# Attention, convolution and a routed expert block on one core: routing split in two parts, an early store tied to a turn, and two projections that change places

## The chip, the core and the metric

The kernel runs on one core of one Trainium2 chip. The metric is the device time of one execution in microseconds (us); less is better. Engines go by their names in the profile: PE (TensorE, the matmuls), PEld (its weight loads), DVE (VectorE), ACT (ScalarE), POOL (GpSimd), SP (SyncE, which here only issues DMAs).

## The reference, cut to what matters

`x` has 8 sequences ("batches" below) of 512 tokens with 256 values each. All data are float32.

```python
x = x + attn_block(layernorm(x))
    # q, k, v = projections; ctx = causal softmax attention, 16 heads of 16
    # q2 = conv1d(ctx, width 3); ctx2 = causal attention(q2, k, v); out projection
x = x + ffn_block(layernorm(x))

def ffn_block(x):
    h = x + attention(rmsnorm(x))            # rotary causal attention, 16 heads of 16
    t = rmsnorm(h)
    probs = softmax(t @ w_router)            # 8 experts
    topw, topi = top_k(probs, 2); topw /= sum(topw)
    return h + sum over the two experts of topw * expert(t)   # silu(t wg) * (t wu) @ wd, hidden 704
```

So each batch passes three causal attentions, and each token then goes to its two best experts.

## The kernel before, in words

**Tiles and stages.** A batch is 4 tiles of 128 tokens. The eight batches are taken in four pairs, p = 0 to 3 (batches 2p and 2p+1). A pair runs six attentions one after the other: first, second, third attention, each for the one batch and then for the other. One attention is 9 steps. A step is 16 score matmuls into two PSUM tiles `sc` (line 1212), two exponentials on ACT from `sc` to `pr` (L1219), the causal mask on POOL (L1227), and, some steps later, the products with the values (L1142). There are only two `sc` tiles, so the scores of a step wait for the exponentials of the step before. After the last expert rows are known, a second phase runs the experts over sorted rows (L742 to L805).

**The order is written out by hand.** Two steps make a turn; a pair has 27 turns (`TURNS`), and turn t+k below is turn 27p+k. Everything that is not attention (projections, convolution, norms, routing) is a "unit" that `plan` puts into a turn. A turn emits: step A; due products with values; the mask; one row transfer (`send`); the "mid" follow-ups; the units of `small_units` and `first_units`; step B; its mask; a transfer; the "late" follow-ups; then the units of `units`; the "end" follow-ups. PE, ACT, DVE and POOL keep exactly that order in their queues. SP's order is left to a scheduler, which issues DMAs when it thinks they can start.

**Normalising an attention.** When a half (`ch`) of an attention has its sums in PSUM, ACT copies them (L1159), SP sends three DMAs (`r<-cs` twice, L1167; `cs<-cs`, L1168), and a turn later DVE does two reciprocals (L1172), two products (L1173) and, for a first attention, the four `differences` for the convolution (L1394 to L1397). For `ch` 0 that comes as a "mid" follow-up, ahead of `small_units`.

**Routing.** For a batch: `logits` (L1571) puts logits in PSUM and copies them to `lT` (L1579). `route` transposes them back (PE, L1585), and then is one chain on DVE: maximum and difference (L1593, L1594), the exponential on ACT (L1595), and then the sums, the two picks (`pick_largest`, L1240 to L1244), `both` (L1603) and the weights (L1604 to L1610). `slots` needs `both`: two matmuls (L1624, L1625) and 16 DVE instructions (L1627 to L1639). Routing of the batches of pair p-1 falls into pair p: `before0` in turns t+1 (`route`) and t+2 (`slots`), `before1` in t+7 and t+10. In t+2 the unit `h` follows `slots`: two groups of matmuls with `wo` (L1041), each followed by an addition on DVE (L1545), one on POOL (L1546) and two squares on ACT (L1548), which write into the same PSUM tile. All these PSUM tiles come from `mm_tile`, which has two banks and takes them in turn.

**The other units named here.** `k(ch)` is a projection (L1052) that ACT takes out of PSUM with two instructions (L1342); `values(half)` is one (L1070) that DVE takes out with two (L1088); both for the next batch, `next0`, in turns t+10 and t+11. `normed2` is ACT (L1480). `conv` is matmuls L1406 with L1415 on ACT and L1420, L1424 on DVE. `xn` (L1323) is the normalised input of the next batch; its transposes are L1292.

**Stores.** `store` (L1266) writes a batch's rows to `out`. For the last batch, 7, it is called early, in `stats` (turn t+20 of p = 2), before anything else touches `out` for that batch; its rows were loaded by a DMA (L679) that `fetch_next` of batch 6 issues (turn t+3 of p = 2).

## Time and profile before

| what | value |
|---|---|
| median of 3 runs | 1439.34 us (1436.92 to 1440.64) |
| the profiled execution: its time | 1439.65 us |
| its span in the trace | 1437.7 us |
| mean granted PE clock | 0.989 |
| PE busy | 1385.2 us, 96% |
| PE weight loads busy | 900.1 us, 63% |
| DVE, ACT, POOL busy | 734.2, 725.7, 579.7 us (51%, 50%, 40%) |
| mean busy share of DMA queues | 15.1% + 5.4% + 0.6% |

The profile is of one execution. Its span runs from the first to the last instruction; 1.95 us of the execution's time lie around it. Lines of the timeline give start, duration, engine, line, operation, tiles, and in brackets how long the engine was idle before and on whom it waited. Matmul ends are modelled, so a wait inside a group of matmuls counts as busy in part; the start of the next group tells the loss. "PEclk" in the table of stretches is the granted PE clock, as a share of full speed.

### The profile page before, as it was taken

To read this page: it belongs to the slowest core of one execution; us is meant where nothing else is said; L and a number is where in the kernel's file an instruction comes from. 1 tells how busy PE (TensorE), PEld (TensorE's weight loads), DVE (VectorE), ACT (ScalarE), POOL (GpSimd) and SP (SyncE) were. 2 spreads that over 40 slices of the span, in tenths; PEclk is the share of its full clock that TensorE was granted. 3 is DMA by queue.
4 is the path that set the end of the run, shared out by engine and by line. 5 is a ranking of instruction groups with operands and counts; after the bars stand their busy time and mean duration, and the time that the engine had idled before them with its cause. 6 is when DMAs were issued, how large, how long until landed. Compare 5 with 4: busy or idle time off the path is not lost. (4 is left out here: it accounts for less than half of the span.)

```text
span 1437.7 us, 32181 instructions
## 1 busy us (share of the span) xinstructions
PE 1385.2 (96%) x13476; PEld 900.1 (63%) x13476; DVE 734.2 (51%) x1458; ACT 725.7 (50%) x1175; POOL 579.7 (40%) x621
## 2 busy tenths in 40 slices
PE   8999999999999899999999999999999999999995
PEld 5566565666565566565565666666766767677673
DVE  5745877675977665976576855322222222222221
ACT  4777786776786676786776883211121111211110
POOL 3334333646333546333655345433324233332321
PEclk9999999999999999999999999999999999999998
DMA  5122122201001201010212022323131313232200
GB/s 148 58 89 83 60 85 69 83 32 57 13 32 45 94 35 58 13 51 31 100 60 71 24 78 101 124 63 112 45 108 61 97 60 103 76 98 81 82 20 17
DMA packets 62842, 97.63 MB, mean 68 GB/s; under 512 B 13516, under 2 KB 39064, under 8 KB 62688
## 3 DMA queue, kind: packets, MB, share of 16 engines
q1 hardware_dynamic: 52608, 69.74, 15.1%
q0 software_dynamic: 10080, 25.74, 5.4%
q8 instruction: 108, 1.77, 0.5%
q14 instruction: 46, 0.38, 0.1%
HBM read 46.06 MB, written 32.61 MB: 55 GB/s over the span
## 5 line engine op out<-in xcount | busy, mean ns | idle before, releaser
L1219 ACT ACTIVATE pr<-sc 128x1024 f32<-128x1024 f32 x432 | 418.8, 1023 | 153.0 <-PE sc L1212 149.3
L1227 POOL TENSOR_TENSOR pr<-pr,seen 128x512 f32<-128x512 f32 (+1 forms) x216 | 256.7, 1189 | 409.9 <-ACT pr L1219 409.8
L764 PE MATMUL pgu<-xgT,gu 128*128 128x384 f32 x1056 | 345.8, 487 | 2.2 <-DVE hT L779 1.6
L764 PEld LDWEIGHTS pgu<-xgT,gu 128*128 128x128 f32 x1056 | 200.0, 190 | 137.0 <-DVE hT L779 2.2
L778 ACT ACTIVATE sg<-pgu 128x384 f32<-128x384 f32 x120 | 58.8, 490 | 413.0 <-PE pgu L764 404.6
L1142 PE MATMUL av<-pr,va 64*32 64x512 f32 (+7 forms) x6144 | 218.9, 407 | 0.0
L1212 PE MATMUL sc<-qT,kT 32*128 32x320 f32 (+7 forms) x2048 | 192.4, 436 | 8.3 <-ACT pr L1219 6.2
L788 PE MATMUL po<-dn,hT 128*128 128x256 f32 x864 | 190.9, 379 | 2.0 <-issue 2.0
L779 DVE TENSOR_TENSOR hT<-sg,pgu 128x384 f32<-128x384 f32 x120 | 66.4, 554 | 247.2 <-ACT sg L778 243.2
L805 POOL DMA_INDIRECT out_dram<-so_far,xg x72 | 72.4, 1006 | 287.8 <-DVE so_far L795 222.1
L1172 DVE RECIPROCAL r<-r 128x256 f32<-128x256 f32 x96 | 167.5, 1744 | 20.5 <-DMA r<-cs 20.4
L1142 PEld LDWEIGHTS av<-pr,va 64*32 64x32 f32 x6144 | 113.4, 106 | 102.5 <-issue 73.7
L788 PEld LDWEIGHTS po<-dn,hT 128*128 128x128 f32 x864 | 162.4, 190 | 23.9 <-issue 2.4
L1212 PEld LDWEIGHTS sc<-qT,kT 32*128 32x128 f32 x2048 | 116.9, 184 | 82.7 <-ACT pr L1219 31.2
L795 DVE SCALAR_TENSOR_TENSOR so_far<-po,xg,so_far 128x256 f32<-128x256 f32 x72 | 34.8, 484 | 151.5 <-PE po L788 147.2
L1212 PE MATMUL sc<-q2T,kT 32*128 32x512 f32 (+7 forms) x1024 | 95.0, 434 | 1.3 <-ACT pr L1219 0.9
L750 POOL DMA_INDIRECT so_far<-out_dram,xg x72 | 74.0, 1028 | 53.7 <-issue 51.9
L1212 PEld LDWEIGHTS sc<-q2T,kT 32*128 32x128 f32 x1024 | 58.1, 184 | 34.5 <-issue 15.0
L1648 POOL DMA_INDIRECT xtab<-rows,slot x64 | 64.6, 1009 | 32.1 <-DVE pick L1637 15.6
L1052 PE MATMUL mm<-xT,wqkv_sb 128*128 128x512 f32 x128 | 62.7, 616 | 1.5 <-DVE xmT L1298 1.2
L1052 PE MATMUL mm<-xaT,wqkv_sb 128*128 128x512 f32 x128 | 61.3, 612 | 2.0 <-DVE xaT L1298 2.0
L1406 PE MATMUL mm<-terms,conv_sb 128*128 128x256 f32 x256 | 62.7, 390 | 0.0
(178 smaller groups left out, 1363.2 us busy)
## 6 DMA issues: line engine op xcount, KB each, us to landing
r<-cs SPq DMA_DIRECT2D x96, 128.0 KB
xtab<-pad SPq DMA_DIRECT2D x24, 397.5 KB
xg<-xtab SPq DMA_DIRECT2D x24, 397.5 KB
gu<-in_wg_dram SPq DMA_DIRECT2D x18, 352.0 KB
cs<-cs SPq DMA_DIRECT2D x48, 128.0 KB
dn<-in_wd_dram SPq DMA_DIRECT2D x9, 640.0 KB
gu<-in_wu_dram SPq DMA_DIRECT2D x18, 320.0 KB
out_dram<-x SPq DMA_DIRECT2D x9, 512.0 KB
```

The lines of the kernel that those rows point to most:

```text
L750: nc.gpsimd.indirect_dma_start(out=so_far[:, s, :], out_offset=None, in_=out, in_offset=token_of(xg, s), bounds_check=B * S - 1, oob_is_er ...
L764: nc.tensor.matmul(ps, gu[d][:, n0 : n0 + P], xgT[:, d, :], start=(d == 0), stop=(d == DC - 1),)
L779: nc.vector.tensor_mul(hT[k], sg, pu)
L788: nc.tensor.matmul(po, hT[k][:, s * P : (s + 1) * P], dn[:, k, :], start=(k == 0), stop=(k == NK - 1),)
L805: nc.gpsimd.indirect_dma_start(out=out, out_offset=token_of(xg, s), in_=so_far[:, s, :], in_offset=None, bounds_check=B * S - 1, oob_is_er ...
L1052: nc.tensor.matmul(ps, w[:, d, n0 : n0 + P], srcT[:, d, :S], start=(d == 0), stop=(d == DC - 1),)
L1142: nc.tensor.matmul(av[i][g * HP : (g + 1) * HP, j * KB :], v[rows, j, ch * G + g, :], pr[rows, g, at : at + n], start=(j == 0), stop=(j == ...
L1172: nc.vector.reciprocal(r[:, half], r[:, half])
L1212: nc.tensor.matmul(sc[:, g - g0, at : at + S - j * KB], kT[r0 : r0 + HP, ch, j], qT[r0 : r0 + HP, ch, j * KB : S], start=True, stop=True,)
L1219: nc.scalar.activation(pr[:, g0 : g0 + 2], sc, AF.Exp, scale=SCALE)
L1227: nc.gpsimd.tensor_tensor(diag, diag, seen.unsqueeze(1).unsqueeze(1).to_broadcast([P, G, len(parts), KB]), ALU.mult,).ins
L1648: nc.gpsimd.indirect_dma_start(out=xtab, out_offset=bass.IndirectOffsetOnAxis(ap=slot[:, c, k : k + 1], axis=0), in_=rows[:, c, :], in_off ...
```

## The change

Three things. `route` is split: `logits_back` stays where `route` was and copies the transposed logits to SBUF (`lg`), and `route` goes one turn later, in `small_units`, that is between step A and step B and after the "mid" follow-ups. In the same place `h` is put ahead of `slots`. The early store of batch 7 gets a dependency on the latest mask on POOL, so that SP can't issue it before its turn. `k(0)` and `values(1)` of `next0` change places (t+10, t+11). For batches 6 and 7, routed at the end, `logits_back` and `route` follow one another.

```diff
+        def not_yet(sent, reason):
+            data = mybir.DependencyInfo(mybir.DependencyClass.Sync, mybir.DependencyReason.DATA)
+            tc.add_manual_dep(sent, masked[-1].name, data, reason=reason)
...
-                    self.store()
+                    not_yet(self.store(), "in its turn")
...
-            def route(self):
-                b, rows = self.b, self.rows
+            def logits_back(self):
                 pl = mm_tile()
                 nc.tensor.transpose(pl[:, :P], self.lT, ident)
-                logits = pl[:, :P].rearrange("p (c e) -> p c e", e=HP)[:, :, :NE]
+                self.lg = small.tile(full, F32, tag="lg", name="lg", bufs=1)
+                nc.vector.tensor_copy(
+                    self.lg, pl[:, :P].rearrange("p (c e) -> p c e", e=HP)[:, :, :NE]
+                )
+
+            def route(self):
+                b, rows, logits = self.b, self.rows, self.lg
...
-            plan(t + 1, before0, "route")
+            plan(t + 1, before0, "logits_back")
+            plan(t + 2, before0, "route", among=small_units)
             plan(t + 1, before1, "normed2", 2, 3)
+            plan(t + 2, before1, "h", 0, 1)
             plan(t + 2, before0, "slots")
-            plan(t + 2, before1, "h", 0, 1)
...
-            plan(t + 7, before1, "route")
+            plan(t + 7, before1, "logits_back")
+            plan(t + 8, before1, "route", among=small_units)
...
-            plan(t + 10, next0, "k", 0)
+            plan(t + 10, next0, "values", 1)
             plan(t + 10, before1, "slots")
-            plan(t + 11, next0, "values", 1)
+            plan(t + 11, next0, "k", 0)
```

In the order of the changed kernel's instructions, each routing has one DVE instruction more (the copy to `lg`, eight in all). In t+8 the whole chain of `route` stands behind the normalising of `ch` 0 (L1172 to L1397) on DVE, and its exponential stands on ACT between the exponentials of step A and those of step B; before, both stood ahead of them. In t+2 the order on PE is `h`, then `slots`, and the two slots matmuls there wait for ACT as well as for DVE. SP's queue has the store of batch 7 some 22 DMAs later, just ahead of the `r<-cs` that starts at 613.67 us in the trace of before; nothing else moves on SP, and nothing on POOL.

More of the change, by code (lines that the diff above doesn't have):

```diff
@@ L922, in fill @@
             written.append(sent)
-            data = mybir.DependencyInfo(mybir.DependencyClass.Sync, mybir.DependencyReason.DATA)
-            tc.add_manual_dep(sent, masked[-1].name, data, reason="one by one")
+            not_yet(sent, "one by one")
         order = wp.tile([P, NE], F32, tag="order", name="order")
@@ L1265, in store @@
                 b = self.b
-                nc.sync.dma_start(
+                return nc.sync.dma_start(
                     out[b * S : (b + 1) * S, :].rearrange("(c p) d -> p c d", p=P), self.xb
-                )
+                ).ins
             def tile(self, shape, tag, name):
@@ L1674, in fast_path @@
         busy = set()
-        NO_MATMULS = ("stats", "fetch_next", "normed", "normed2", "rms", "bias")
+        NO_MATMULS = ("stats", "fetch_next", "normed", "normed2", "rms", "bias", "route")
         def unit(t, what, *args):
@@ L1889, in fast_path @@
                 if part == 3:
+                    plan(n_turns - 1, batches[B - 2], "logits_back")
                     plan(n_turns - 1, batches[B - 2], "route")
@@ L1959, in fast_path @@
             go_on(parts[0])
+            t.logits_back()
             t.route()
```

## The prediction

> **What bounds the kernel now.** The page gives PE 96% of the span, every other engine 51% or less: PE's order sets the end, and an edit is worth what PE stands still. So I read PE's waits next (line, whom it waited for: us in all, times, longest):

> ```profile
> PE sc L1212 <- ACT pr L1219: 7.1, 7, 2.3
> PE mm L1292 <- DVE va L1088: 4.7, 2, 4.4
> PE mm L1624 <- DVE both L1603: 1.7, 3, 0.9
> ```

> Then the timeline around each. In turn t+2 of p = 2:

> ```profile
> 455.56 0.23 ACT L1595 ACTIVATE prob<-prob 128x32 f32<-128x32 f32 x1 [1.77 <-DVE prob L1594]
> 455.70 1.08 ACT L1480 ACTIVATE rows<-x,shift,rstd 128x256 f32<-128x256 f32 x2
> ...
> 456.68 1.91 ACT L1219 ACTIVATE pr<-sc 128x1024 f32<-128x1024 f32 x2
> 457.74 2.04 PE L1212 MATMUL sc<-qT,kT 32*128 32x512 f32 x8 [2.25 <-ACT pr L1219]
> 458.94 1.14 DVE L1603 TENSOR_TENSOR both<-pick,pick 128x32 f32<-128x32 f32 x1
> 460.61 5.39 PE L1041 MATMUL mm<-wo_sb,c 128*128 128x256 f32 x16
> 464.21 0.69 DVE L1545 TENSOR_TENSOR rows<-rows,mm 128x512 f32<-128x512 f32 x1 [0.23 <-PE mm L1041]
> 465.93 1.22 PE L1212 MATMUL sc<-qT,kT 32*128 32x448 f32 x16
> ```

> ACT stands 1.77 us before the routing's exponential, with the attention's exponentials queued behind it; PE then waits 2.25 us for an `sc` tile. Around the early store, p = 2:

> ```profile
> 475.48 0.38 SPq L1266 DMA_DIRECT2D out_dram<-x  x1
> 477.91 0.47 SPq L1168 DMA_DIRECT2D cs<-cs  x1
> 481.73 0.43 DVE L1173 TENSOR_TENSOR cx<-cs,r 128x256 f32<-128x256 f32 x1 [2.05 <-DMA cs<-cs]
> 488.27 1.94 PE L1292 MATMUL mm<-ident,xn 128*128 128x128 f32 x8 [4.39 <-DVE va L1088]
> ```

> SP holds the store until the batch's load (issued 471.10) has landed; `cs<-cs` waits behind it, so DVE is late, and then PE. Last, the stretches of 3.4 us (width, PE, PEld, DVE, ACT, POOL busy, then granted clock):

> ```profile
> 454.00:457.40 3.40, 1.48 (x60) 0.84 (x40) 2.79 (x12) 1.84 (x4) 0.00 (x0) 1.00 0.02 5
> 457.40:460.80 3.40, 2.69 (x13) 1.26 (x14) 3.02 (x12) 3.02 (x4) 1.31 (x1) 1.00 0.00 0
> 460.80:464.20 3.40, 3.40 (x9) 2.65 (x9) 2.73 (x18) 0.11 (x1) 0.72 (x1) 0.50 0.01 2
> ```

> After a stall PE's clock is halved for such a stretch: `h` takes 5.32 us to the next scores instead of 3.84 (twice the 1.92 of such a group, L1041 at 215.55 us). That is 1.5 us on top of a stall.

> **1. Turn t+2 (three times).** From the products before step B to the next turn's scores PE took 13.65 us (from 240.33), 12.46 (453.47) and 11.0 (670.58). Work alone: products 1.94, scores 1.07, `h` 3.84, slots 0.46: 7.31. The edit takes ACT's first wait away but builds another. For p = 2, from T = 453.47:
> - `normed2` follows ACT's last check (ends T+0.3), so step A's exponentials start at T+1.2 (before T+3.2). Step B's scores come as their tiles get free (T+2.2, T+3.2), and `h` at T+4.25 (second tile + 1.07). PE has the first half of `h` done at 6.2, the second at 8.1.
> - The routing's exponential now waits for step A's two, to T+3.05. The chain goes on 0.26 later (as 455.56 to 455.82) and takes 3.3 us to `both` and 0.95 more to its end, without blocks. A DVE product with both inputs in SBUF stops while POOL masks (L1603 above: 1.14 us instead of 0.19, three of eight). Mask A falls in (+0.7) and probably mask B (0.72 long, I take +0.45). End of `route`: T+8.7.
> - DVE adds `h` only then. The slots matmuls take the bank of `h`'s first half, so they wait for its squares: 1.78 us from the addition's start (464.21 to the end of the second square, 465.99). T+10.5, plus 0.46: next scores at T+11.0.

> PE is idle from T+8.1 to T+10.5, 2.4 us. Gains: 13.65-11.1 = 2.55 (p = 1 the same times), 12.46-11.0 = 1.45, and for p = 3, where the check ends 0.5 earlier, 11.0-10.5 = 0.5: **4.5 us**. Without any block, 8.0; the blocks are the unknown.

> **2. The early store.** Without it p = 2 should run as p = 1, which has the same store of batch 2p-2 and load just before: from the products to the projection after the transposes 9.12 us (482.78 to 491.90) against 3.46 (271.05 to 274.51): **5.7 us**, with its halved clock. At its new place SP waits for a mask of t+20, before 600 us, and the next `r<-cs` starts at 613.67: nothing waits. If the 512 KB still met a normalising there, a delay like the 2.4 us of `cs<-cs` above could come back.

> **3. Keys and values.** In t+11 ACT has two checks, then `k`'s two instructions (1.45 us), then the exponentials:

> ```profile
> 312.29 1.45 ACT L1342 ACTIVATE kT<-mm,bk_sb,parity 128x512 f32<-128x512 f32 x2
> 312.56 2.01 PE L1142 MATMUL av<-pr,va 64*32 64x384 f32 x64
> ...
> 313.61 1.95 ACT L1219 ACTIVATE pr<-sc 128x1024 f32<-128x1024 f32 x2
> ...
> 314.70 2.04 PE L1212 MATMUL sc<-q2T,kT 32*128 32x512 f32 x8
> ```

> Products take 2.14 instead of 1.94 and scores 1.97 instead of 1.07: 1.1 lost, 0.95 regained (the second tile still comes 0.15 late). p = 0 loses 1.36 but its `differences` end 3.7 us after the turn's scores, so `values` leaves its bank only at +5.1 while `k` wants it at +4.25: 0.4 regained. Sum **2.3 us** (1.9 to 3.3). `k` on ACT behind step B is covered: it is ready 2.0 us after its matmuls start, and the next exponentials are not.

> **4. Turn t+8 (three times): a new wait.** Before, in p = 1:

> ```profile
> 293.24 0.23 ACT L1595 ACTIVATE prob<-prob 128x32 f32<-128x32 f32 x1 [2.37 <-DVE prob L1594]
> ...
> 296.80 1.94 ACT L1219 ACTIVATE pr<-sc 128x1024 f32<-128x1024 f32 x2 [1.47 <-PE sc L1212]
> ...
> 298.55 1.75 DVE L1172 RECIPROCAL r<-r 128x256 f32<-128x256 f32 x1
> 298.56 1.35 PE L1212 MATMUL sc<-q2T,kT 32*128 32x512 f32 x8
> ```

> The 2.37 us of ACT cost nothing here: step A's scores start at 292.13, and exponentials follow scores by 1.25 us anyway (295.54 to 296.80). Afterwards the normalising (298.55 to 304.33, 5.78 us) goes first on DVE. Its DMAs are there (issued 287.73 and 290.37; elsewhere they need 2.6 and 2.0 us), so it runs from 293.1 to 298.9; L1593 and L1594 to 299.3; ACT's exponential to 299.5. Behind it on ACT stand step B's exponentials, 2.65 us late, and PE's next scores wait for their tiles: **3 x 2.65 = 8.0 us lost**. It would be less only if DVE had the five normalising microseconds free earlier, which the DMA times exclude; a mask that blocks a product could add 0.9.

> **5. The rest.** Eight copies to `lg` (about 0.2 us each) lie beside matmuls; in the expert phase the two routings stand beside `pgu` groups. In t+5 of p = 1 the 0.35 us that PE waits for DVE goes, since the store and load come earlier against the scores: +0.4 (0 to 0.7).

> **6. The clock.** The six new stalls (2.4 to 2.65 us) can halve it again. The row: stretches with 1.20, 2.21 and 2.69 us of PE work led to half clock, one with 1.48 did not. The half-clock spells start at 245.79, 460.83, 488.14 and 675.87 us, whole multiples of 3.413 us apart: where a boundary falls decides. Sliding a 3.41 us stretch along each new stall, about half of the positions hold under 1.4 us of work: three of six, 1.5 us each: **4.5 us lost**. [...]

> **Sum.** 4.5 + 5.7 + 2.3 + 0.4 - 8.0 - 4.5 = 0.4 us gained, from the profiled 1439.65 (span 1437.7 and 1.95 around it): **1439 us**, which is also the median of the runs, 0.3 lower.

> **Rivals.**
> - *The new stalls stay short or keep the clock.* For: they are shorter than the 4.39 us after which the clock fell for certain, and one stretch with 1.48 us of work did no harm. Against: the three half-clock stretches after 2.3 us and less. No lost clock: 1434.7; also no blocks in t+2 and the upper bound of 3: 1439.65 - (8.0 + 5.7 + 3.3 + 0.7 - 8.0) = 1430. I put it at 1432.
> - *Slower: the clock pays double.* At 245.80 half clock lasted 6.8 us, and cost 2.7. Place: after each stall in t+2 and t+8. Six times 2.7 is 16.2 against a gain of 4.9: 1451. It decides for slower (above 1443.7) from (4.9 + 4.1)/6 = 1.5 us per stall.
> - *The store's edit doesn't do it:* the load of batch 7 alone delays `cs<-cs` in p = 2. Against: p = 1 has a load there. 1439 + 5.7 = 1445.

> **How the numbers follow.** About 0.3% (4.3 us) is what a measurement of this kernel can tell from no change. Forecast 0.45 (its own range 1435 to 1443.5), first rival 0.36, second 0.13, third 0.06. Faster 0.36, same 0.45, slower 0.19. The range reaches from all the first rival's bounds, 1430, to the third, 1445; it leaves out most of the second.

> **What would show it.** Right: no wait of PE for `va` near 480 us; PE waiting for ACT ahead of the slots matmuls in t+2, 2.4 us; ACT idle 2.6 us on DVE before L1595's successor in t+8; scores of 1.2 us in t+11; some half-clock stretches after these. Wrong: the exponential in t+8 following step A's at once, or full clock throughout.

## The result, and the profile after

The changed kernel takes **1443.41 us** (median of 20 runs, 1437.34 to 1447.49), the kernel before 1439.09 us beside it (20 runs, 1435.74 to 1442.72): ratio 1.0029, 95% interval 1.0017 to 1.0040. It is 4.3 us slower where 1439 us, no change, was forecast. The profiled execution took 1446.37 us (span 1444.4), 3 us above its median, so sums made from its trace come out somewhat too large.

Line numbers are 4 higher than before up to the routing (scores L1216, exponentials L1223, mask L1231, `h` L1045) and 9 higher within it (exponential L1604, `both` L1612, slots L1633). The line of busy times on its page, and PE's waits:

```profile
PE 1388.4 (96%) x13476; PEld 897.0 (62%) x13476; DVE 735.5 (51%) x1466; ACT 725.9 (50%) x1175; POOL 579.0 (40%) x621
```

```profile
PE mm L1633 <- ACT mm L1552: 7.5, 3, 2.7
PE sc L1216 <- ACT pr L1223: 7.2, 8, 2.0
```

The wait of 4.4 us for `va` is gone. In its place stand three waits of the slots matmuls for `h`'s squares. PE has the same 13476 matmuls and yet 3.2 us more busy time: matmuls at half clock take longer (below, the same scores 2.22 us instead of 1.22) and count as busy. In turn t+2 of p = 2 the timeline now reads:

```profile
457.21 0.22 ACT L1604 ACTIVATE prob<-prob 128x32 f32<-128x32 f32 x1
...
458.42 3.72 PE L1045 MATMUL mm<-wo_sb,c 128*128 128x256 f32 x16
...
462.99 1.28 DVE L1549 TENSOR_TENSOR rows<-rows,mm 128x512 f32<-128x512 f32 x2
...
464.81 0.63 PE L1633 MATMUL mm<-both,before 128*128 128x32 f32 x2 [2.67 <-ACT mm L1552]
...
465.80 2.22 PE L1216 MATMUL sc<-qT,kT 32*128 32x448 f32 x16
```

ACT no longer idles before the routing's exponential. But DVE adds `h` only at 462.99, when the routing is through; PE has finished `h` by 462.1 and stands for 2.67 us. The scores behind it then take 2.22 us instead of 1.22: half clock. Turn t+8 of p = 1:

```profile
288.61 1.74 DVE L1176 RECIPROCAL r<-r 128x256 f32<-128x256 f32 x1
...
294.82 0.23 ACT L1604 ACTIVATE prob<-prob 128x32 f32<-128x32 f32 x1 [3.77 <-DVE prob L1603]
294.95 1.92 ACT L1223 ACTIVATE pr<-sc 128x1024 f32<-128x1024 f32 x2
...
296.01 2.96 PE L1216 MATMUL sc<-q2T,kT 32*128 32x512 f32 x8 [1.67 <-ACT pr L1223]
...
298.90 3.66 PE L1146 MATMUL av<-pr,va 64*32 64x384 f32 x64
```

DVE goes through the normalising (288.61 to 294.38) before it reaches the routing; ACT waits 3.77 us for that, with the exponentials of step B behind; PE waits for those. Its scores then take 2.96 us (1.35 before), with a wait for the second tile among them, and the products, at half clock, 3.66 (2.01 before).

How far each stage moved is read from the starts of the same matmul groups in the two traces. "Waits alone" is what the stage shows in a run in which no half clock fell into it (the runs with extra matmuls, below; for t+8 run 4 in p = 3, run 3 in the others); "clock" is the rest. "Elsewhere" is read in the changed kernel itself. The kernel before has five half-clock stretches of its own; what their going is worth is part of the first two rows.

| stage (all pairs together) | predicted | waits alone | clock |
|---|---|---|---|
| t+2, products to next scores | -4.5 | -4.5 (-2.69, -1.27, -0.56) | +4.5 |
| near 480 us, p = 2 | -5.7 | -5.95 | |
| exchange, t+11 | -2.3 | -2.7 (-1.1, -0.9, -0.7) | |
| t+4 to t+6 | -0.4 | -2.0 | |
| t+8 | +8.0 | +7.6 (2.42, 2.42, 2.72) | +6.3 |
| t+10 of p = 3, half clock at 744.1 us | 0 | | +1.6 |
| elsewhere | 0 | +2.3 | |
| lost clock | +4.5 | | +12.4 |
| sum | -0.4 | -5.3 | +7.1 with the waits |

The profiled times differ by 6.7 us. "Elsewhere" holds 1.67 us near 565 us in p = 2, where PE waits for DVE's products because a `cs<-cs` landed late (runs 3 and 4 don't have it), and 0.6 us before the first turn.

So two things had to be explained. **The clock:** the theory is that each new wait of PE is paid again in half clock behind it, so that matmuls put into a wait win time although they shorten nothing; the rival is that the loss is in the waits themselves or in later ones, and extra matmuls then win nothing. **The stall near 480 us:** the prediction's theory is that the early store held `cs<-cs` back, so undoing that one edit brings the stall back; the rivals are that the load does it, or the row transfers, and that the new order in t+2 only moved them against PE.

### The profile page after: what moved, and what is told of

It is laid out like the page before. It is cut to its first block, busy times and chain, and to the rows that moved or that the text cites. A ratio compares the mean times of both kernels' runs of the same rounds, so it can differ in the third digit from the quotient of the medians.

```text
span 1444.4 us, 32182 instructions
## 1 busy us (share of the span) xinstructions
PE 1388.4 (96%) x13476; PEld 897.0 (62%) x13476; DVE 735.5 (51%) x1466; ACT 725.9 (50%) x1175; POOL 579.0 (40%) x621
## 3 DMA queue, kind: packets, MB, share of 16 engines
q8 instruction: 108, 1.77, 0.5%
## 5 line engine op out<-in xcount | busy, mean ns | idle before, releaser
L1223 ACT ACTIVATE pr<-sc 128x1024 f32<-128x1024 f32 x432 | 418.9, 1023 | 156.0 <-PE sc L1216 155.5
L1231 POOL TENSOR_TENSOR pr<-pr,seen 128x512 f32<-128x512 f32 (+1 forms) x216 | 256.0, 1185 | 410.3 <-ACT pr L1223 400.8
L1146 PE MATMUL av<-pr,va 64*32 64x512 f32 (+7 forms) x6144 | 222.6, 417 | 0.0
L1216 PE MATMUL sc<-qT,kT 32*128 32x320 f32 (+7 forms) x2048 | 192.7, 437 | 3.5 <-ACT kT L1523 1.9
L1216 PEld LDWEIGHTS sc<-qT,kT 32*128 32x128 f32 x2048 | 116.6, 185 | 78.2 <-ACT pr L1223 29.2
L1216 PE MATMUL sc<-q2T,kT 32*128 32x512 f32 (+7 forms) x1024 | 97.4, 442 | 6.1 <-ACT pr L1223 5.8
L1216 PEld LDWEIGHTS sc<-q2T,kT 32*128 32x128 f32 x1024 | 59.4, 187 | 41.4 <-ACT pr L1223 17.2
L1657 POOL DMA_INDIRECT xtab<-rows,slot x64 | 65.0, 1015 | 32.1 <-DVE pick L1646 15.5
```

The lines of the kernel that those rows point to most:

```text
L1146: nc.tensor.matmul(av[i][g * HP : (g + 1) * HP, j * KB :], v[rows, j, ch * G + g, :], pr[rows, g, at : at + n], start=(j == 0), stop=(j == ...
L1216: nc.tensor.matmul(sc[:, g - g0, at : at + S - j * KB], kT[r0 : r0 + HP, ch, j], qT[r0 : r0 + HP, ch, j * KB : S], start=True, stop=True,)
L1223: nc.scalar.activation(pr[:, g0 : g0 + 2], sc, AF.Exp, scale=SCALE)
L1231: nc.gpsimd.tensor_tensor(diag, diag, seen.unsqueeze(1).unsqueeze(1).to_broadcast([P, G, len(parts), KB]), ALU.mult,).ins
L1657: nc.gpsimd.indirect_dma_start(out=xtab, out_offset=bass.IndirectOffsetOnAxis(ap=slot[:, c, k : k + 1], axis=0), in_=rows[:, c, :], in_off ...
```

## The experiments

Ratios are to the kernel before, on the same chip, with 95% intervals. It had medians of 1438.4, 1439.2 and 1438.9 us beside the three groups of runs, so plain differences between medians are good to about 1 us.

**1. The second routing back in its old place.** Only the part in t+8 is undone.

```diff
-            plan(t + 8, before1, "route", among=small_units)
+            plan(t + 7, before1, "route")
```

> The changed kernel with the routing of before1 put back whole into turn t+7 (copy and chain one after the other). Theory, the wait in t+8: ACT no longer stands on the routing behind DVE's normalising, so three stalls of 2.65 us and the half-clock spells after them go: 8 us plus about 2 us of clock each, 13 to 14 us less than the changed kernel, near 1430 us, below the kernel before. In the trace PE goes from the scores of 1212/1216 for step B of t+8 to those of t+9 without a wait on ACT. Rival, the loss lies in t+2 (the slots matmuls waiting for h's squares): within 2 us of the changed kernel.

Measured: 1430.74 us (6 runs), ratio 0.9950 (0.9936 to 0.9965). t+8 stands where it stood before, and the time is the one that the theory gave. That one line costs 12.7 us of 1443.4: more than its own waits, 7.6.

**2. The first routing back instead.** `route` of before0 returns to t+1, `slots` ahead of `h`; t+8 stays changed.

```diff
-            plan(t + 2, before0, "route", among=small_units)
-            plan(t + 2, before1, "h", 0, 1)
+            plan(t + 1, before0, "route")
             plan(t + 2, before0, "slots")
+            plan(t + 2, before1, "h", 0, 1)
```

> The changed kernel with before0's routing back in t+1 and slots ahead of h again in t+2; t+8 stays as changed. Theory, the wait in t+8: this part of the edit is close to even (about 4 us gained on waits, most of it lost again to half clock), so between 2 us faster and 4 us slower than the changed kernel. Rival, the loss lies in t+2: 5 us or more faster than the changed kernel.

Measured: 1447.12 us (6 runs), 1.0056 (1.0039 to 1.0073), 3.7 us above the changed kernel. The part in t+2 is worth something. Near 480 us the gain shrinks from 5.95 to 3.20, with a wait of PE for `va` of 2.73 us, although the store's edit is still in: the first sign that the store was not the cause.

**3 and 4. Extra matmuls into the waits.** Five matmuls that nobody reads fill PE's wait in t+2 (run 3) or stand ahead of the late scores in t+8 (run 4). They shorten no dependency; they only keep PE at work.

```diff
+        def filler():
+            for n in (3, 2):
+                ps = ps_sc.tile([P, 2, 512], F32, tag="sc", name="filler")
+                for _ in range(n):
+                    nc.tensor.matmul(
+                        ps[:, 0, :256], wqkv_sb[:, 0, :P], wqkv_sb[:, 1, :256], start=True, stop=True
+                    )
...
             plan(t + 2, before1, "h", 0, 1)
+            if before0 is not None:
+                units[t + 2].append(filler)
             plan(t + 2, before0, "slots")
```

In run 4 the five matmuls stand in t+8 behind `conv` (1, 0) and write into the bank that the next unit will take.

> The changed kernel with five matmuls of 128x128 by 256 columns (2.4 us) more in t+2, between h and slots, into score tiles that are free there; their results are overwritten. They fill the wait of 2.4 us with PE work and change no dependency. Theory, the clock: the half-clock spells after t+2 go, 1 to 4 us less than the changed kernel although PE has 36 passes more. Rival, half clock costs nothing because PE would wait anyway: the same as the changed kernel or up to 1 us slower.

> The changed kernel with the same five matmuls more in t+8, after conv(1,0) and before the next scores, into the matmul bank that is free there; their results are overwritten. Theory, the clock: the wait for ACT stays (2.65 us three times) but full clock follows it: about 6 us less than the changed kernel. Rival, half clock costs nothing: the same as the changed kernel or up to 1 us slower.

Measured: run 3 1434.68 us (12 runs), 0.9980 (0.9968 to 0.9991), **8.7 us less** than the changed kernel, with 30 matmul records more in the trace (13506); run 4 1437.51 us (12 runs), 0.9994 (0.9979 to 1.0009), 5.9 us less. In run 3 the next scores start where they would have started anyway:

```profile
458.38 2.32 PE L1701 MATMUL filler<-wqkv_sb 128*128 128x256 f32 x10
...
461.21 0.41 PE L1633 MATMUL mm<-both,before 128*128 128x32 f32 x2 [0.51 <-ACT mm L1552]
...
461.77 1.22 PE L1216 MATMUL sc<-qT,kT 32*128 32x448 f32 x16
```

From the start of `h` (454.82) to these scores it is 6.95 us, against 7.38 in the changed kernel (458.42 to 465.80). What the fillers change in t+2 is the clock. The stretches of 3.4 us (width, PE, PEld, DVE, ACT, POOL busy, granted clock) of the changed kernel around the wait:

```profile
460.85:464.27 3.42, 1.29 (x6) 0.79 (x5) 3.02 (x12) 0.53 (x3) 0.51 (x1) 1.00 0.00 0
464.27:467.68 3.41, 2.87 (x20) 2.05 (x20) 1.50 (x11) 1.40 (x6) 1.80 (x2) 0.50 0.20 68
467.68:471.09 3.41, 3.41 (x29) 1.45 (x24) 2.10 (x10) 2.98 (x6) 1.91 (x2) 0.50 0.36 107
```

and of run 3:

```profile
458.82:462.24 3.42, 2.91 (x17) 2.17 (x19) 2.01 (x7) 1.93 (x8) 2.09 (x2) 1.00 0.01 2
```

One stretch with 1.29 us of PE work is followed by two at half clock; with 2.91 us of work none follows here. Run 3's trace has one half-clock spell in p = 1 to 3 (mean granted clock 0.994), the changed kernel's six (0.987), two of them twice as long. That is more than the fillers alone explain: they stand in t+2 only, yet in p = 1 and p = 2 the waits of t+8, as long as in the changed kernel (2.42 us), keep the clock too. So part of the 8.7 us comes from t+8, and why these waits kept the clock in this trace isn't shown. In run 4 the late scores come no earlier (t+8 moves by +2.42, +2.42, +2.72), but no half clock follows them; four spells elsewhere stay, three of them behind t+2 (mean granted clock 0.990).

**5. The store's edit undone** in the changed kernel.

```diff
-                    not_yet(self.store(), "in its turn")
+                    self.store()
```

> The changed kernel with the early store as before (no dependency on a mask). Theory: the wait of PE near 480 us comes back as before, 5.7 us more than the changed kernel with its half-clock spell, about 1449 us. Rival, the load alone delays the transfer: within 1.5 us of the changed kernel.

Measured: 1445.75 us (11 runs), 1.0054 (1.0036 to 1.0073). The early store is back between `r<-cs` and `cs<-cs` (issued 471.77), and the stretch near 480 us still gains 5.95 us. The transposes (L1296) never wait for `va`. By its trace the store's edit is worth nothing at this place. The median, 2.3 us above the changed kernel, fits neither forecast (5.7, or within 1.5); run 12 repeats the test with the clock nearly full.

**6. The exchange undone.** `k(0)` back to t+10, `values(1)` to t+11.

> The changed kernel with k(0) in t+10 and values(1) in t+11 again. Theory: scores of t+11 wait for ACT again; 2.3 to 3.3 us more than the changed kernel. Rival, what is gained there is waited for in t+12: within 1 us.

Measured: 1447.61 us (7 runs), 1.0059 (1.0037 to 1.0081): 4.2 us above the changed kernel by the medians. The trace gives t+11 +0.13, 0, 0 against before, so the exchange itself is worth 2.7; the other 1.5 us lie within the scatter of the runs (1437 to 1447 us for the changed kernel).

**7. Both routings back**: before, with the copy to `lg`, the store's edit and the exchange.

> The changed kernel with both routings back in their old turns and slots ahead of h; only the copy to lg, the store and the exchange of keys and values are left of the change. Theory: the waits of before in t+2 stay and those of t+8 don't arise, so the kernel before less 6 us for the store and 3 for the exchange: 1429 to 1431 us, about equal to the kernel with only before1's routing back. Rival, the split of before0's routing is worth its 4.5 us with its clock: 4 us or more above that kernel.

Measured: 1438.09 us (12 runs), 0.9992 (0.9975 to 1.0009), 7 us above what the theory gave. t+11 gains its 2.7. But the stall near 480 us is all there, though the early store is gone. Its timeline (SPq, POOL and DVE lines that carry it):

```profile
470.94 0.38 SPq L679 DMA_DIRECT2D x<-in_x_dram  x1
...
471.42 1.11 SPq L1171 DMA_DIRECT2D r<-cs  x2
...
477.55 1.01 POOL L1657 DMA_INDIRECT xtab<-rows,slot  x1 [0.15 <-issue]
477.71 0.47 SPq L1172 DMA_DIRECT2D cs<-cs  x1
477.72 1.75 DVE L1176 RECIPROCAL r<-r 128x256 f32<-128x256 f32 x1 [3.41 <-DMA r<-cs]
...
481.60 0.43 DVE L1177 TENSOR_TENSOR cx<-cs,r 128x256 f32<-128x256 f32 x1 [2.13 <-DMA cs<-cs]
...
488.14 1.94 PE L1296 MATMUL mm<-ident,xn 128*128 128x128 f32 x8 [4.42 <-DVE va L1092]
```

`r<-cs` is issued 0.48 us behind the load of 512 KB and takes 6.3 us; `cs<-cs` is issued 0.16 us behind a row transfer and takes 3.9, where 2.6 and 2.0 are usual. Two suspects, then, neither of them the store; experiments 9 and 10 take one away each.

**8. The slots a turn later**: run 1, with before0's `slots` at the end of t+3, out of the way of `h`'s squares.

> before1's routing whole in t+7, before0's split as changed, and before0's slots moved on to the end of t+3. Theory, the bank: in t+2 PE no longer waits for h's squares ahead of slots; the next scores follow h at once, with some 0.6 us of waiting left ahead of q(1). About 2 us less in each of three turns and no half clock after them: 1420 to 1424 us. Rival, the wait only moves: the same as with before1's routing back alone, 1431 us.

Measured: 1431.73 us (7 runs), 0.9946 (0.9925 to 0.9967), no better than run 1. t+2 gains more (-5.76, -4.57, -3.62 us), but 1.5 and 1.2 us come back later in p = 1, 1.97 in p = 2, and near 480 us only 1.78 are gained instead of 5.95. The wait moves.

**9. Row transfers held**: kernel 7, with the transfers of before0 going out from t+5 on.

```diff
-                to_send.extend(rows_ready)
-                rows_ready.clear()
+                if n % TURNS not in (2, 3):
+                    to_send.extend(rows_ready)
+                    rows_ready.clear()
```

> The kernel before with the store in its turn and the projections exchanged (1438.1 us; PE waits 4.4 us for va near 480 us in p = 2, and its clock is halved afterwards) plus one thing: the row transfers of before0 go out from t+5 on instead of t+3, so that none stands on POOL just ahead of r<-cs or cs<-cs of the first half. Theory R, the row transfers delay the normalising (cs<-cs 3.9 us instead of 2.0): PE's wait falls to 2.5 us or less, 2 to 5 us gained, 1433 to 1436. Theory L, the load just ahead of r<-cs does it: the wait stays above 3 us and the time at 1437 to 1439.

**10. The load held**: kernel 7, with the load behind a mask of t+4.

```diff
-            plan(t + 3, next0, "fetch_next")
...
+            plan(t + 4, next0, "fetch_next")
...
-                load_x(self.b + 1)
+                sent = load_x(self.b + 1)
+                if self.b % 2 == 0:
+                    not_yet(sent, "after the sums")
```

> The same base (1438.1 us), with the load of the batch after next held until the mask of t+4's step B, behind cs<-cs, instead of 0.5 us ahead of r<-cs; the row transfers stay. Theory L: r<-cs takes 2.6 us instead of 6.3, PE's wait near 480 us falls below 1 us, the half clock after it goes, about 5 us gained, 1433. Theory R: r<-cs or cs<-cs still takes 4 us or more, the wait stays above 2.5 us, 1436 to 1438.

Measured: 9 gives 1436.05 us (12 runs), 0.9977 (0.9963 to 0.9992); 10 gives 1430.79 us (6 runs), 0.9936 (0.9914 to 0.9959). In 9 `r<-cs` still takes 5.7 us behind the load, `cs<-cs` 2.0, and PE's wait falls to 0.93 us; the stretch gains 5.0, some of it lost again later. In 10 (its lines stand 2 higher than in kernel 7):

```profile
471.69 1.11 SPq L1173 DMA_DIRECT2D r<-cs  x2
...
474.24 0.47 SPq L1174 DMA_DIRECT2D cs<-cs  x1
...
475.76 1.74 DVE L1178 RECIPROCAL r<-r 128x256 f32<-128x256 f32 x1
...
482.69 0.38 SPq L679 DMA_DIRECT2D x<-in_x_dram  x1
```

`r<-cs` is through in 2.6 us, no wait of PE is left, and the stretch gains the same 5.95 us as in the changed kernel. Both theories were half right: of the 5.6 us by which the two DMAs are late in kernel 7, 3.1 stay without the row transfers (run 9), but only 0.9 without the load (run 10, `cs<-cs` 2.9), so the two don't simply add; with either gone PE's wait falls below 1 us. Why `r<-cs` is late behind the load is not shown: the runs give these times alone.

**11 and 12. The parts that pay, together.** 11 is run 1 with the fillers of run 3; 12 is the same without the store's edit.

> The changed kernel with the route of before1 back in t+7 (1430.7 us) and the five extra matmuls in t+2's wait. If half clock after the t+2 stalls is what was left there (spells of 3.41 us at 250 and 462 us in that kernel), they go: 1427, 3 to 4 us less. If the fillers only add work: 1430.7 or more.

> The run before this one without the early store's dependency, with little left of the clock to blur it. If the store's edit is worth nothing here: within 1.5 us of that run. If it is worth what the prediction gave it: 5.7 us more, with a wait of PE for va near 480 us.

Measured: 11 1426.80 us (6 runs), 0.9909 (0.9892 to 0.9927); 12 **1424.33 us** (6 runs, 1423.18 to 1425.67), 0.9892 (0.9875 to 0.9910), the fastest kernel here. Its span is 1421.2 us. Both profiles have full clock until the last 14 us (mean granted clock 0.995 and 0.996), and both gain 5.95 us near 480 us, 12 without the store's edit. Its median is 2.5 us below that of run 11, where 1.5 at most was expected; in run 5 the same step went 2.3 us the other way. So no gain of the store's edit is seen, and certainly not 5.7 us; the five idle matmuls are worth 3.9 us to run 1. The busy times on the page of kernel 12:

```profile
PE 1379.5 (97%) x13506; PEld 898.7 (63%) x13506; DVE 732.3 (52%) x1466; ACT 725.2 (51%) x1175; POOL 580.5 (41%) x621
```

PE has 30 matmul records more than before and is busy 5.7 us less, and none of its matmuls before the last 12 us ran at half clock.

## Why the prediction was wrong

Step by step, by its own numbers:

- **Step 1, t+2: right.** 11.1, 11.0 and 10.5 us were predicted from the products to the next scores; without half clock they are 10.96, 11.2 and 10.4, together 4.5 us gained as said. The chain too: PE waits for the squares of `h` behind the routing on DVE, 2.67 us for a predicted 2.4, and two products (L1607 0.87 us, L1610 0.62 us, instead of 0.19) were blocked during the two masks (457.45 to 458.71 and 459.77 to 460.49), as it had assumed. In the trace of before, 51 of 52 products of two SBUF tiles that start during a mask, at least 0.25 us before its end, are prolonged, and none of the 47 there with one input in PSUM.
- **Step 2, the early store: right sum by luck, wrong cause.** The 5.95 us came, but not from the store: kernel 7 has the store's edit and the stall, runs 5 and 12 have neither. The step that failed is "SP holds the store until the batch's load (issued 471.10) has landed; `cs<-cs` waits behind it". SP did hold it (issued 4.4 us behind the load; in the changed kernel two such loads take 4.3 and 3.9 us), but in before `r<-cs` had landed only at 477.9, by which time the store was out (issued 475.48); `cs<-cs` was released by `r<-cs`, as the waits of SP's queue in the kernel before show (455 to 484 us, the line below). What was late was `r<-cs`, 0.48 us behind the load, and `cs<-cs` next to a row transfer. The third rival, "the load of batch 7 alone", named one of the two, and its price was taken off by step 1's edit: with `h` ahead of `slots` the residual's addition on POOL, and with it store, load and normalising, comes earlier against PE. In kernel 7 PE reaches the projection's transposes (L1296) 12.3 us after `r<-cs` was issued (471.42 to the end of the products at 483.7), in the changed kernel 15.5 (470.65 to 486.14). There `r<-cs` also takes only 3.0 us (6.3 in kernel 7) and `cs<-cs` 2.3 (3.9); it is issued 1.5 us behind the load, and no row transfer goes out just ahead of either. That it is the first routing's part, its later turn together with `h` ahead of `slots`, and not the copy or the exchange, follows from runs 2 and 7; which of the two it is, and the link by way of POOL, is read from the traces and was not tried alone.

```profile
SPq L1168 <- DMA r<-cs: 2.0, 1, 2.0
```

- **Step 3, the exchange: right**, 2.7 for 2.3 (1.9 to 3.3).
- **Step 4, t+8: right.** 2.42, 2.42 and 2.72 us for a predicted 2.65, by the predicted chain.
- **Step 5: too low.** 2.0 us instead of 0.4, also in p = 2 and p = 3.
- **Step 6, the clock: the step that decides the miss.** 4.5 us were put in, "three of six, 1.5 us each". In the profiled execution half clock followed five of the six stalls (no listed wait of PE in them longer than 2.7 us), in seven stretches of 3.41 us instead of three, with an eighth at 744.1 us behind a wait of 0.5 us that the kernel before has too: 12.4 us in all. That it is the clock, runs 3 and 4 show: matmuls that shorten nothing give 8.7 and 5.9 us back. The other terms together came out as forecast, 5.3 us gained for 4.9. This execution lies 3 us above the median, so nearer 9 us are usual (an estimate from these two numbers). What failed is the count by "under 1.4 us of work": the prediction's own row had half clock behind 2.21 and 2.69 us of work, and in t+8 of the changed kernel it came behind 1.75 (293.60 to 297.02), 1.95 and 2.37 us. No run shows a limit of 1.4 us, or that the place of a stretch's boundary decides; both were the author's estimate from the stretches of before. The other half of the miss is the price: two of the spells lasted 6.83 us, not 3.41.

The second rival described what happened, though not its size: half clock after the stalls in t+2 and t+8, slower from 1.5 us per stall. The profiled execution shows (4.5 + 6.3) / 6 = 1.8 us per stall, between its 2.7 and the forecast's 0.75. Before had shown the double spell once in four; the changed kernel shows it twice in six.

Much of the scatter between runs goes with the clock too: over the 20 runs of the changed kernel the mean granted clock goes from 0.984 to 0.991, and the time falls by about 12 us per 0.01 of clock (correlation -0.80); a whole hundredth of 1440 us would be 14. Kernel 12 has 0.996 in the median, and its six runs lie within 2.5 us.

## What to carry to other kernels

A short wait of a busy PE had two prices here: its own length, and the half clock behind it; 10.8 us were lost to half clock behind 15.1 us of new waits (7.5 in t+2, 7.6 in t+8). So a few matmuls that nobody reads, placed in a wait that can't be removed, are worth trying (8.7 us less in run 3). Before a unit is moved behind another engine's long block, follow what is queued behind its first cross-engine hop: ACT's one small exponential (0.23 us, after a wait of 3.77) held all the scores of the next step, 2.42 to 2.72 us. And a late DMA is to be explained by its own issue time and what was issued just before it: a store that happens to stand there may be innocent (in run 7 the store is held and PE still waits 4.42 us; with the load held, in run 10, `r<-cs` takes 2.6 us instead of 6.3).
